# First block of an attention and convolution kernel: exponentials taken before the mean is known, their factor applied to the values and the sums

## The chip, the cores and the metric

The kernel runs on one core of a Trainium2 chip. The metric is the device time of one execution in microseconds (us). The kernel before took 1884.59 us, the median of four runs between 1883.92 and 1884.70. Engines are called TensorE (PE), VectorE (DVE), ScalarE (ACT), GpSimd (POOL) and SyncE (SP), which here only issues transfers.

## The reference

The input x has 8 images of 64 channels and 64 x 64 pixels, all in 32-bit floats. Layer 0 is an attention over the 4096 pixels of each image, with a second, unary softmax; layer 1 is a sum of three convolutions of signs (1x1, 3x3, 5x5) with a gate. What matters here is layer 0:

```python
q = einsum('oc,bcn->bon', wq, xf) + bq        # k and v alike
q = q - q.mean(axis=2);  k = k - k.mean(axis=2)
sim = softmax(einsum('bcn,bcm->bnm', q, k) / 8, axis=2)
out = einsum('bnm,bcm->bcn', sim, v)
unary = softmax(einsum('bc,bcm->bm', q_mean, k))
x = x + out + einsum('bcm,bm->bc', v, unary)
```

Inside a softmax over the keys m, a term that depends on the query n alone changes nothing, so the mean of k can be left out, and the scores are x_m . (M x_n - M mean(x)) / 8 with one product matrix M of wq and wk. Per key m, leaving out the mean multiplies every exponential by the same factor exp(x_m . M mean(x) / 8).

## The kernel before

**Tiling.** Two images lie side by side on the 128 partitions (a pair), so there are four pairs; x of a pair is a tile of 128 x 4096. The queries of a pair are cut into 8 blocks of 512 (`QB`); the 4096 keys into 32 tiles of 128. For each block and each key tile j three things happen. `scores` (L575) does four 64x64 matmuls of x against the queries q into a PSUM tile of 128 x 1024 (`ps`), and ScalarE takes the exponential of it into a tile `e`. `weighted` (L600) adds four matmuls of the value tile v against `e` to the accumulators `acc`. `summed` (L617) adds `e` to the running sums `es` on VectorE; key tiles 5, 11, 17 and 23 are instead added in DRAM by a GpSimd transfer. The convolutions of earlier blocks are mixed in between.

**Buffers.** PSUM holds two score tiles (`ps_s`), two accumulator banks (`ps_a`) and two small banks (`ps_m`, tag m). Five `e` tiles rotate (`ep`, bufs=5): an exponential needs the buffer of the tile five before it, which its weighted sum and its running sum must have left.

**Order.** Everything stands in a hand-written order (`manual_schedule`), and each engine runs its own instructions in the order in which the program lists them. `attend` (L1316) goes through the blocks: in step i it lists the scores of tile i, then the weighted sum and the running sum of tile i - 1, and then the extra steps that `plan` has put at i. Tiles whose exponentials exist already (the list `early`) skip the scores. `values` (L409) makes four value tiles at a time, with one more column for the logits of the unary softmax; `unary_part` (L435) uses them.

**The start.** x of the first pair comes in four quarters on the queues of SP and ACT (L77). TensorE meanwhile multiplies a matrix of ones (`warm`, L158), then makes M (`projection`, L160) and a key bias. When the first quarter is there, the first block's queries are made (`queries`, L536), copied without the mean by VectorE and ScalarE (`early_queries`, L346), and the scores of key tiles 0 and 1 are taken, but not their exponentials. The sums of x (`mean_part`, L296) run on VectorE and ScalarE; `mean_scores` (L312) turns them into M mean(x), `mean_scores_out` gives `mx` and `minus_mean_scores` `nmx`. `early_values` makes value tiles 0 to 3. `early_columns` (L372) makes, for each key of tiles 0 to 3, the mean's term and the unary logit; `early_exponentials` (L393) takes the exponentials of tiles 0 and 1 with the mean's term as bias, in two halves each, one per image. `mean_to_queries` (L405) subtracts the mean from the queries for the tiles after that, and `mix((first, 1), None)` makes block 1's queries.

**The end.** Sums and other denominators are tested against limits by `check` (L515), whose results are added up in `fit`; if any fails, a slower general path runs behind the main one.

Of the kernel before, what the change touches and what calls it, by code (L numbers as in the profile page):

```python
# [26 lines left out]
P = 128  # L27
C = 64
# [16 lines left out]
LOW, HIGH = 1e-20, 1e20  # L45


@with_exitstack
def conv_seq_kernel(ctx, tc, x, wqv, wk, wv, w1, w3, w5, wtap, gw, out):
# [41 lines left out]
    xt = load_x("0", slice(0, P), (nc.sync, nc.scalar, nc.sync, nc.sync))  # L91
    nc.sync.dma_start(out=wv_s, in_=wv)
# [29 lines left out]
    fit = cp.tile([P, 2, n_pairs * (NQ + 1) + 1], F32, tag="fit", name="fit")  # L122
# [47 lines left out]
    def vectors():  # L170
        nc.vector.tensor_scalar(inv, rv, BN_EPS, None, ALU.add)
        nc.vector.tensor_scalar(bv2, bv_s, 2.0, None, ALU.mult)
        nc.vector.tensor_scalar(ngb, gb_s, -1.0, None, ALU.mult)
        nc.scalar.activation(inv, inv, AF.Sqrt)

        nc.scalar.activation(lim[:, 2:3], ones[:, 0:1], AF.Exp)

# [102 lines left out]
    class Pair:  # L280
# [3 lines left out]
        def __init__(self, name, xt):  # L284
# [5 lines left out]
            self.lines = None  # L290
# [21 lines left out]
        def mean_scores(self):  # L312

            self.pm = m_tile(f"pm_{self.name}")
            for b in range(2):
                nc.tensor.matmul(
                    self.pm[img[b], 0:1], mm[img[b], img[b]], self.xm[img[b]], start=True, stop=True
                )
# [33 lines left out]
        def early_values(self):  # L352

            pv = self.pv = acc_banks(f"pv_{self.name}_e")
            for i in range(4):
                for h in range(2):
                    for b in range(2):
                        nc.tensor.matmul(
                            pv[b][img[h], i * C : (i + 1) * C],
                            self.x[img[b], bass.ds(i * P + h * H, H)],  # L360
                            self.wx[img[b], 0:C],
# [3 lines left out]

# [1373 lines left out]
```

## Time and profile before

| What | Value |
|---|---|
| median of four runs | 1884.59 us |
| the profiled execution, its time | 1884.04 us |
| its span on the core | 1882.2 us |
| granted TensorE clock | 1.0 |
| TensorE matmul busy | 1872.1 us, 99% |
| VectorE busy | 1609.2 us, 85% |
| ScalarE busy | 1265.4 us, 67% |
| exponentials of one tile (128x1024) | 1.02 us |
| running sum of one tile (128x1024) | 1.21 us |
| multiply-add on 128x512 from memory (L735) | 0.75 us |

The profile is of one execution. A row of the order of time gives the start and the duration in us, engine, line, operation, what it writes and reads, the count of instructions merged, and in brackets how long the engine was idle before and what released it. A row of the chain of waits gives the start, the duration and the instruction that the end of the kernel waited for at that time. A 32-bit matmul appears as two rows. The rows by half microseconds end with the granted clock, the share of the DMA engines and GB/s. Lines L... are those of the kernel before; the changed kernel has other numbers.

### The profile page before, as it was taken

The numbers are of one execution on the slowest core, as the hardware profiler recorded it, in microseconds if no ns is written. First come the engines' busy times: TensorE is split into PE (matmuls) and PEld (weight loads), VectorE is DVE, ScalarE is ACT, GpSimd is POOL, SyncE is SP. The second block draws the span as 40 slices with busy tenths as digits, with TensorE's granted clock in tenths as the row PEclk, the third lists the DMA queues.
The fourth block names the chain that finished last, engine by engine and source line by source line (L and its number), as shares of the span: only waits on it lengthen the run. The fifth ranks groups of instructions, "written<-read, shape, count | busy, mean of one in ns | idle before, by whom it ended". The sixth has DMA issues, their size and how long they took to land.

```text
span 1882.2 us, 51531 instructions
## 1 busy us (share of the span) xinstructions
PE 1872.1 (99%) x22076; PEld 794.4 (42%) x22076; DVE 1609.2 (85%) x2550; ACT 1265.4 (67%) x1622; POOL 130.4 (7%) x176
## 2 busy tenths in 40 slices
PE   9999999999999999999999999999999999999998
PEld 4344344443344434444434443444433444444446
DVE  7888888889888888888888898888888888888898
ACT  6666776666666676666666667666666666666664
POOL 0000000000000000000000000000000000000000
PEclk9999999999999999999999999999999999999999
DMA  4234333333333533333233343333332333333321
GB/s 126 66 62 104 82 66 72 67 58 72 68 71 78 128 81 78 67 70 71 52 81 66 89 118 83 69 70 69 72 67 59 78 75 91 89 64 78 71 51 56
DMA packets 74004, 142.81 MB, mean 76 GB/s; under 512 B 10540, under 2 KB 42152, under 8 KB 73640
## 3 DMA queue, kind: packets, MB, share of 16 engines
q0 software_dynamic: 22320, 81.27, 23.2%
q1 hardware_dynamic: 51160, 57.58, 10.4%
q8 instruction: 174, 2.85, 0.6%
q10 hardware_dynamic: 288, 0.60, 0.1%
q14 instruction: 62, 0.51, 0.1%
HBM read 39.27 MB, written 89.78 MB: 69 GB/s over the span
## 4 chain that ended last, share of the span: by engine, by line
PE 96%; DVE 2%; DMA 1%; issue 0%; ACT 0%; SPq 0%; DVEq 0%; ACTq 0%
PE ps L584 45%; PE acc L609 45%; PE z L979 2%; DVE es L627 1%; PE pv L416 1%; PE pq L565 1%; PE z L1110 0%; DMA es<-e 0%; PE z_5e L979 0%; DMA x<-in_x 0%; ACT e L597 0%; DMA e_parts<-es 0%; PE su L709 0%; PE z L1069 0%; DVE vu_lines L800 0%
## 5 line engine op out<-in xcount | busy, mean ns | idle before, releaser
L597 ACT ACTIVATE e<-ps 128x1024 f32<-128x1024 f32 (+1 forms) x1030 | 1047.5, 1017 | 564.0 <-PE ps L584 547.2
L627 DVE TENSOR_TENSOR es<-es,e 128x1024 f32<-128x1024 f32 (+1 forms) x841 | 1018.9, 1212 | 192.1 <-ACT e L597 177.6
L584 PE MATMUL ps<-q,x 64*64 64x512 f32 (+2 forms) x8448 | 1088.3, 577 | 0.8 <-DVE q L349 0.8
L609 PE MATMUL acc<-e,v 64*64 64x512 f32 (+2 forms) x8432 | 1084.3, 577 | 1.2 <-ACT e L597 1.0
L609 PEld LDWEIGHTS acc<-e,v 64*64 64x64 f32 x8432 | 333.0, 131 | 548.0 <-ACT e L597 314.9
L584 PEld LDWEIGHTS ps<-q,x 64*64 64x64 f32 x8448 | 356.2, 133 | 485.3 <-issue 263.7
L648 POOL DMA_DIRECT2D es<-e x93 | 80.1, 861 | 903.6 <-ACT e L597 598.5
L1049 DVE SCALAR_TENSOR_TENSOR sb<-pt,sb 128x256 f32<-128x256 f32 x174 | 65.9, 419 | 0.0
L979 PEld LDWEIGHTS <-wc 64*64 64x64 bf16 x3364 | 58.7, 106 | 1.7 <-issue 0.8
L648 POOL DMA_DIRECT2D es<-es x31 | 26.6, 857 | 438.6 <-DVE es L627 438.6
L625 DVE TENSOR_TENSOR es<-e,e 128x1024 f32<-128x1024 f32 (+1 forms) x31 | 37.7, 1216 | 17.2 <-ACT e L597 17.2
L979 PE MATMUL z<-ec,wc 64*64 64x128 bf16 x1392 | 51.4, 217 | 0.0
L979 PE MATMUL z<-t,wc 64*64 64x128 bf16 x1392 | 51.0, 216 | 0.1
L773 ACT ACTIVATE s<-x,wqv_s 128x512 bf16<-128x512 f32 (+2 forms) x66 | 46.2, 702 | 0.0
L1012 ACT ACTIVATE pt<-z,frac 128x256 f32<-128x256 f32 (+1 forms) x58 | 30.6, 577 | 16.9 <-PE z L979 16.9
L646 POOL DMA_DIRECT2D es<-e x31 | 17.5, 563 | 334.3 <-ACT e L597 323.1
L635 DVE COPY o<-acc 128x512 f32<-128x512 f32 (+1 forms) x32 | 22.0, 687 | 9.4 <-PE acc L609 9.3
L1023 DVE TENSOR_TENSOR pt<-pt 128x384 f32<-128x384 f32 x58 | 29.6, 552 | 0.0
L416 PEld LDWEIGHTS pv<-wx,x 64*64 64x64 f32 x992 | 21.5, 134 | 16.1 <-issue 8.6
L735 DVE SCALAR_TENSOR_TENSOR x<-x,ou,x 128x512 f32<-128x512 f32 (+2 forms) x33 | 24.3, 736 | 1.2
L663 DVE TENSOR_TENSOR e_parts<-e_parts 128x512 f32<-128x512 f32 x31 | 21.3, 688 | 3.6 <-DMA e_parts<-es 3.6
L424 ACT COPY v<-pv 128x512 f32<-128x512 f32 x31 | 18.2, 586 | 8.7 <-PE pv L416 8.7
(207 smaller groups left out, 889.9 us busy)
## 6 DMA issues: line engine op xcount, KB each, us to landing
es<-e POOLq DMA_DIRECT2D x124, 512.0 KB, 5.1
es<-es POOLq DMA_DIRECT2D x31, 512.0 KB, 5.3
e_parts<-es SPq DMA_DIRECT2D x124, 128.0 KB, 3.0
r<-rc SPq DMA_DIRECT2D x62, 128.0 KB, 2.8
out<-sb SPq DMA_DIRECT2D x29, 256.0 KB, 2.3
x<-in_x SPq DMA_DIRECT2D x24, 256.0 KB, 4.4
ec<-t SPq DMA_DIRECT2D x29, 99.0 KB, 4.4
xc<-in_x SPq DMA_DIRECT2D x30, 72.0 KB
```

Source lines behind the costliest of these rows:

```text
L416: nc.tensor.matmul(pv[img[h], b, i * w : (i + 1) * w], self.x[img[b], bass.ds((4 * g + i) * P + h * H, H)], self.wx[img[b], 0:w], start=Tr ...
L584: nc.tensor.matmul(ps[img[h], b, i * w : (i + 1) * w], self.x[img[b], bass.ds((n * j + i) * P + h * H, H)], self.q[qb][img[b], cols], star ...
L597: nc.scalar.activation(e, ps[:, :, 0 : n * w], AF.Exp, scale=1.0 / 8.0)
L609: nc.tensor.matmul(self.acc[qb][h][img[b], 0:w], self.v[img[h], t, img[b]], e[img[h], b, at : at + w], start=(t == 0), stop=(t == NK - 1),)
L625: begin.tensor_tensor(self.es[qb], self.first, e, ALU.add)
L627: nc.vector.tensor_tensor(self.es[qb], self.es[qb], e, ALU.add)
L648: nc.gpsimd.dma_start(out=out, in_=e, accum_op=ALU.add)
L773: nc.scalar.activation(sy[n][0][:, rows, pad : pad + HH], self.x2[qb][:, r0 * HH : r1 * HH].rearrange("p (h w) -> p h w", w=HH), AF.Sign, ...
L979: nc.tensor.matmul(z[img[b], :].rearrange("p (q w) -> p q w", w=HH), wc[k][img[h], n, c * C : c * C + C], src[:, first : first + step + 1 ...
L1012: nc.scalar.activation(out, z, AF.Identity, scale=frac[:, by : by + 1])
L1023: nc.vector.tensor_tensor(self.pairs[:, :, :, r, :], t[:, 0:3, 0], t[:, 0:3, 1], op)
L1049: nc.vector.scalar_tensor_tensor(out, x, by, out, ALU.mult, ALU.add, **gap)
```

## The change

The first part of x is loaded as 512 columns and the whole of x in six parts, all issued by SP; the value weights come on the ACT queue ahead of them. The exponentials of key tiles 0 to 2 are taken as soon as their scores are there, from queries without the mean; that of tile 3 stands behind the first factors in ScalarE's order. The factor of each key, exp of the mean's term, is taken later (`early_factors`), multiplied into a copy `vf` of value tiles 0 to 3 (`early_weights`), which the weighted sums of these tiles read, and into the running sums (`early_sum`). One check on the factors is added. The scores of key tile 4 are listed in the start as well. All sums of x but one run on VectorE; the last part's sum goes into the mean's matmul as a second column. Block 1's queries move to step 6 of block 0, the weight loads behind the factors, and the copies of the value weights to GpSimd. Of the warm-up matmuls 6, 2 and 3 stay of 6, 6 and 3. Blank lines are left out of the diff.

```diff
--- before.py
+++ after.py
@@ -43,6 +43,8 @@
 LOW, HIGH = 1e-20, 1e20
+EARLY = 4
+FACTOR = 1e8
@@ -88,8 +90,12 @@
     w_tap = xp.tile([P, FIRST[3], C], F32, tag="v", name="w_tap")
     nc.scalar.dma_start(out=wqv_s, in_=wqv)
     nc.sync.dma_start(out=wk_s, in_=wk)
-    xt = load_x("0", slice(0, P), (nc.sync, nc.scalar, nc.sync, nc.sync))
-    nc.sync.dma_start(out=wv_s, in_=wv)
+    nc.scalar.dma_start(out=wv_s, in_=wv)
+    xt = x_tile("0")
+    X_PARTS = [(0, 1), (1, 2), (2, 4), (4, 6), (6, 7), (7, 8)]
+    X_PARTS = [slice(a * QB, b * QB) for a, b in X_PARTS]
+    for cols in X_PARTS:
+        nc.sync.dma_start(out=xt[:, cols], in_=xf[0:P, cols])
...
@@ -167,13 +173,15 @@
         nc.tensor.matmul(t[:, 0:1], wk_s, bq_s, start=True, stop=True)
         nc.vector.tensor_copy(kb, t[:, 0:1])
+    def variances():
+        nc.vector.tensor_scalar(inv, rv, BN_EPS, None, ALU.add)
+        nc.scalar.activation(inv, inv, AF.Sqrt)
+        nc.scalar.activation(lim[:, 2:3], ones[:, 0:1], AF.Exp)
     def vectors():
-        nc.vector.tensor_scalar(inv, rv, BN_EPS, None, ALU.add)
         nc.vector.tensor_scalar(bv2, bv_s, 2.0, None, ALU.mult)
         nc.vector.tensor_scalar(ngb, gb_s, -1.0, None, ALU.mult)
-        nc.scalar.activation(inv, inv, AF.Sqrt)
-        nc.scalar.activation(lim[:, 2:3], ones[:, 0:1], AF.Exp)
@@ -287,7 +295,7 @@
-            self.lines = None
+            self.lines, self.f, self.vf = None, None, None
         def tile(self, pool, tag, i, shape=(P, QB), dtype=F32):
             return pool.tile(list(shape), dtype, tag=tag, name=f"{tag}_{self.name}_{i}")
@@ -309,13 +317,19 @@
             self.xm = self.tile(sm, "xm", 0, (P, 1))
             nc.vector.tensor_reduce(self.xm, self.xs[:, 0:parts], AX.X, ALU.add)
-        def mean_scores(self):
+        def mean_scores(self, more=()):
             self.pm = m_tile(f"pm_{self.name}")
-            for b in range(2):
-                nc.tensor.matmul(
-                    self.pm[img[b], 0:1], mm[img[b], img[b]], self.xm[img[b]], start=True, stop=True
-                )
+            cols = [self.xm] + [self.xs[:, c : c + 1] for c in more]
+            for i, col in enumerate(cols):
+                for b in range(2):
+                    nc.tensor.matmul(
+                        self.pm[img[b], 0:1],
+                        mm[img[b], img[b]],
+                        col[img[b]],
+                        start=(i == 0),
+                        stop=(i == len(cols) - 1),
+                    )
         def mean_scores_out(self):
             self.mx = self.tile(sm, "mx", 0, (P, 1))
@@ -325,22 +339,24 @@
-        def value_tiles(self):
+        def value_tiles(self, copy=nc.vector.tensor_copy):
             self.v = self.tile(xp, "v", 0, (P, NK, P))
-            wx = self.wx = self.tile(sm, "wx", 0, (P, C + 2))
+            wx = self.wx = self.tile(sm, "wx", 0, (P, C + 1))
             for b in range(2):
-                nc.vector.tensor_copy(wx[img[b], 0:C], wv_s[img[b], img[b]])
-        def value_weights(self, tiles=True):
-            if tiles:
-                self.value_tiles()
-            else:
-                nc.vector.tensor_scalar(
-                    self.wx[:, C + 1 : C + 2], self.pm[:, 0:1], -1.0 / (8 * N), None, ALU.mult
-                )
+                copy(wx[img[b], 0:C], wv_s[img[b], img[b]])
+        def value_weights(self):
+            self.value_tiles()
+            self.unary_weights()
+        def unary_weights(self):
             nc.vector.tensor_tensor(self.wx[:, C : C + 1], self.mx, kb, ALU.add)
+        def factor_weights(self):
+            self.wb = self.tile(sm, "wb", 0, (P, 1))
+            nc.vector.tensor_scalar(self.wb, self.pm[:, 0:1], -1.0 / (8 * N), None, ALU.mult)
         def early_queries(self, qb):
@@ -349,58 +365,79 @@
             nc.vector.tensor_copy(q[img[0]], self.pq[0][img[0]])
             nc.scalar.copy(q[img[1]], self.pq[1][img[1]])
-        def early_values(self):
-            pv = self.pv = acc_banks(f"pv_{self.name}_e")
-            for i in range(4):
+        def early_matmuls(self, to, tiles, weights, at):
+            for i, t in enumerate(tiles):
                 for h in range(2):
                     for b in range(2):
+                        w = weights[img[b]]
+                        n = w.shape[-1]
                         nc.tensor.matmul(
-                            pv[b][img[h], i * C : (i + 1) * C],
-                            self.x[img[b], bass.ds(i * P + h * H, H)],
-                            self.wx[img[b], 0:C],
+                            to[b][img[h], at + i * n : at + i * n + n],
+                            self.x[img[b], bass.ds(t * P + h * H, H)],
+                            w,
                             start=True,
                             stop=True,
                         )
+        def early_values(self):
+            self.pv = acc_banks(f"pv_{self.name}_e")
+            self.early_matmuls(self.pv, range(EARLY), self.wx[:, 0:C], 0)
         def early_values_out(self):
             for b in range(2):
                 nc.scalar.copy(
-                    self.v[:, 0:4, img[b]], self.pv[b][:, 0 : 4 * C].rearrange("p (t c) -> p t c", c=C)
+                    self.v[:, 0:EARLY, img[b]],
+                    self.pv[b][:, 0 : EARLY * C].rearrange("p (t c) -> p t c", c=C),
                 )
-        def early_columns(self, i0):
-            if i0 == 0:
-                self.add = self.tile(sm, "add", 0, (P, 2, 4, 2))
-            pb = misc_banks(f"pb_{self.name}_e{i0}")
-            for i in range(2):
-                for h in range(2):
-                    for b in range(2):
-                        nc.tensor.matmul(
-                            pb[b][img[h], 2 * i : 2 * i + 2],
-                            self.x[img[b], bass.ds((i0 + i) * P + h * H, H)],
-                            self.wx[img[b], C : C + 2],
-                            start=True,
-                            stop=True,
-                        )
+        def early_columns(self, i):
+            if i == 0:
+                self.f = self.tile(sm, "add", 0, (P, 2, EARLY))
+                self.pb = acc_banks(f"pb_{self.name}_e")
+            else:
+                self.pb = misc_banks(f"pb_{self.name}_e")
+            self.early_matmuls(self.pb, range(i, i + 2), self.wb, 0)
+        def early_exponential(self, ps, j):
+            e = ep.tile([P, 2, QB], F32, tag="e", name=f"e_{self.name}_e{j}")
+            nc.scalar.activation(e, ps, AF.Exp, scale=1.0 / 8.0)
+            return e
+        def early_factors(self, i):
             for b in range(2):
-                nc.vector.tensor_copy(
-                    self.add[:, b, i0 : i0 + 2], pb[b][:, 0:4].rearrange("p (t c) -> p t c", c=2)
-                )
-        def early_exponentials(self, ps, j):
-            e = ep.tile([P, 2, QB], F32, tag="e", name=f"e_{self.name}_e{j}")
-            for b in range(2):
-                nc.scalar.activation(
-                    e[:, b, :], ps[:, b, :], AF.Exp, scale=1.0 / 8.0, bias=self.add[:, b, j, 1:2]
-                )
-            return e
+                nc.scalar.activation(self.f[:, b, i : i + 2], self.pb[b][:, 0:2], AF.Exp)
         def early_unary(self):
             self.eu = self.tile(sm, "eu", 0, (P, 2, NK))
-            nc.scalar.activation(self.eu[:, :, 0:4], self.add[:, :, :, 0], AF.Exp)
+            for b in range(2):
+                nc.scalar.activation(self.eu[:, b, 0:EARLY], self.pb[b][:, 2 : 2 + EARLY], AF.Exp)
+        def early_weights(self, i):
+            if i == 0:
+                self.vf = self.tile(fp, "r", "vf", (P, EARLY, P))
+            nc.vector.tensor_tensor(
+                self.vf[:, i : i + 2, :].rearrange("p t (b c) -> p b t c", b=2),
+                self.v[:, i : i + 2, :].rearrange("p t (b c) -> p b t c", b=2),
+                self.f[:, :, i : i + 2].unsqueeze(3).broadcast_to([P, 2, 2, C]),
+                ALU.mult,
+            )
+        def early_sum(self, qb, j, e):
+            if j == 0:
+                self.es[qb] = self.tile(sm, "es", qb, (P, 2, QB))
+            es = self.es[qb]
+            for b in range(2):
+                f = self.f[:, b, j : j + 1]
+                if j == 0:
+                    nc.vector.tensor_scalar(es[:, b, :], e[:, b, :], f, None, ALU.mult)
+                else:
+                    nc.vector.scalar_tensor_tensor(
+                        es[:, b, :], e[:, b, :], f, es[:, b, :], ALU.mult, ALU.add
+                    )
@@ -512,7 +549,12 @@
-        def check(self, r, i, sides=(0, 1)):
+        def check_factors(self):
+            self.check(self.f.rearrange("p b t -> p (b t)"), n_pairs * (NQ + 1) + 1, high=FACTOR)
+        def check(self, r, i, sides=(0, 1), high=None):
             w = r.shape[-1]
             for side in sides:
@@ -525,7 +567,7 @@
                     r,
                     AF.Sign,
                     bias=lim[:, side : side + 1],
-                    scale=1.0 - 2.0 * side,
+                    scale=(1.0, -HIGH / high)[side] if high else 1.0 - 2.0 * side,
                     accum_out=fit[:, side, i : i + 1],
                 )
@@ -600,6 +642,7 @@
         def weighted(self, qb, j, e, part=(slice(0, QB), 1)):
             cols, n = part
             w = cols.stop - cols.start
+            v = self.vf if self.early(qb, j) else self.v
             if j == 0:
                 self.acc[qb] = acc_banks(f"acc_{self.name}_{qb}_{cols.start}")
             for t in range(n * j, n * j + n):
@@ -608,15 +651,21 @@
                     for h in range(2):
                         nc.tensor.matmul(
                             self.acc[qb][h][img[b], 0:w],
-                            self.v[img[h], t, img[b]],
+                            v[img[h], t, img[b]],
                             e[img[h], b, at : at + w],
                             start=(t == 0),
                             stop=(t == NK - 1),
                         )
+        def early(self, qb, j):
+            return self.vf is not None and qb == 0 and j < EARLY
         def summed(self, qb, j, e, dram=False, begin=nc.vector):
-            if dram and j in DRAM_TILES:
+            if self.early(qb, j):
+                self.early_sum(qb, j, e)
+            elif dram and j in DRAM_TILES:
                 self.add_in_dram(qb, e, j == DRAM_TILES[0])
             elif j == 0:
                 self.first = e
@@ -1405,7 +1454,10 @@
                 for i in range(NQ):
                     if i > 0:
                         put(4 * i - 1, pairs[0].values, i)
-                    put(4 * i + 1, pairs[0].unary_part, i)
+                    put(4 * i + 1 if i > 0 else 5, pairs[0].unary_part, i)
+                put(1, pairs[0].early_weights, 2)
+                put(6, lambda: mix((pairs[0], 1), None))
+                put(10, pairs[0].check_factors)
...
@@ -1580,37 +1632,45 @@
     with tc.manual_schedule():
         first = Pair("0", xt)
+        first.value_tiles(nc.gpsimd.tensor_copy)
+        variances()
         warm(6)
         projection()
-        vectors()
         key_bias()
-        warm(6)
-        first.mean_part(0, quarters[0])
+        warm(2)
+        first.mean_part(0, X_PARTS[0])
         first.query_tiles(0, score_tiles)
         for b in range(2):
             first.queries(0, b)
+        warm(3)
+        first.mean_part(1, X_PARTS[1], True)
         first.early_queries(0)
-        early = [first.scores(0, j, exp=False) for j in range(2)]
-        first.mean_part(1, quarters[1], True)
-        first.mean_part(2, quarters[2])
-        for c in range(2):
-            first.mean_part(3 + c, slice(N * (6 + c) // 8, N * (7 + c) // 8), c == 1)
-        first.value_tiles()
+        early = [first.scores(0, j) for j in range(2)]
         first.early_values()
+        early.append(first.scores(0, 2))
+        first.early_values_out()
+        last = first.scores(0, 3, exp=False)
+        for c in range(2, 5):
+            first.mean_part(c, X_PARTS[c])
+        first.mean_sum(5)
+        first.mean_part(5, X_PARTS[5])
+        first.mean_scores((5,))
+        first.factor_weights()
+        first.mean_scores_out()
+        first.mean_to_queries(0)
+        first.early_columns(0)
+        first.early_factors(0)
+        early.append(first.early_exponential(last, 3))
+        first.unary_weights()
+        first.minus_mean_scores()
+        first.early_columns(2)
+        first.early_matmuls(first.pb, range(EARLY), first.wx[:, C : C + 1], 2)
+        first.early_factors(2)
+        early.append(first.scores(0, 4))
+        first.early_unary()
+        first.early_weights(0)
         load_weights()
-        first.mean_sum(5)
-        first.mean_scores()
-        first.mean_scores_out()
-        warm(3)
-        first.early_values_out()
-        first.value_weights(False)
-        first.minus_mean_scores()
-        first.early_columns(0)
-        early = [first.early_exponentials(ps, j) for j, ps in enumerate(early)]
-        first.mean_to_queries(0)
-        first.early_columns(2)
-        first.early_unary()
-        mix((first, 1), None)
+        vectors()
         good = attend([first] + [None] * (n_pairs - 1), early)
```

More of the change, by code (lines that the diff above doesn't have):

```diff
@@ L120, in conv_seq_kernel @@
     rec = cp.tile([P, 8], F32, tag="rec", name="rec")
-    fit = cp.tile([P, 2, n_pairs * (NQ + 1) + 1], F32, tag="fit", name="fit")
+    fit = cp.tile([P, 2, n_pairs * (NQ + 1) + 2], F32, tag="fit", name="fit")
     lim = cp.tile([P, 3], F32, tag="lim", name="lim")
@@ L1529, in attend @@
         nc.vector.tensor_reduce(nb_, fit, AX.XY, ALU.add)
-        nc.vector.tensor_scalar(nb_, nb_, n_pairs * (16.0 * NQ + 2.0) - 16.0 + 2 * QB, None, ALU.is_equal)
+        nc.vector.tensor_scalar(nb_, nb_, n_pairs * (16.0 * NQ + 2.0) - 16.0 + 2 * QB + 4.0 * EARLY, None, ALU.is_equal)
         p.signs_wide(b, 2, r0, r1, None)
```

## The prediction

> **What bounds the kernel now.** I read the page's head first, then the chain of waits, then the order of time of the first 15 us, then the arrival of x.
>
> ```profile
> span 1882.2 us, 51531 instructions
> PE 1872.1 (99%) x22076; PEld 794.4 (42%) x22076; DVE 1609.2 (85%) x2550; ACT 1265.4 (67%) x1622; POOL 130.4 (7%) x176
> PE 96%; DVE 2%; DMA 1%; issue 0%; ACT 0%; SPq 0%; DVEq 0%; ACTq 0%
> ```
>
> TensorE is busy for 99% of the span and carries 96% of the chain. A change at the start is worth what it takes out of the stretch before TensorE runs without gaps, plus the real matmuls that it moves into that stretch. The chain of the first 40 us shows where the gapless stretch begins and what a step costs:
>
> ```profile
> 1.20 5.47 DMA x<-in_x
> 8.56 1.95 PE ps L584 x16
> 12.31 0.52 PE pb_e L381 x16
> 13.76 0.71 PE pq L537 x2
> ...
> 20.53 0.86 PE acc L609 x8
> 21.39 0.86 PE ps L584 x8
> 26.54 0.46 PE pv L416 x32
> 27.00 0.91 PE ps L584 x8
> ```
>
> From 13.76 us matmuls follow each other; a tile's scores or its weighted sum costs 0.86 us, a group of four value tiles 0.46. Check: between 13.76 and 27.00 (the start of score tile 8) stand block 1's queries, weighted sums 0 to 6, scores 2 to 7 and two value groups: 13 x 0.86 + 2 x 0.46 + about 0.86 = 12.96 of 13.24 us, so only 0.28 us is gap. The order of time shows what the stretch before consists of:
>
> ```profile
> 4.45 0.29 DVE L163 COPY mm<-mm_p 128x128 f32<-128x128 f32 x1 [3.43 <-PE mm_p L162]
> 6.72 1.08 PE L537 MATMUL pq<-x,mm 64*64 64x512 f32 x4 [0.31 <-DMA x<-in_x]
> 7.87 0.58 ACT L350 COPY q<-pq 64x512 f32<-64x512 f32 x1 [1.30 <-PE pq L537]
> 10.47 0.85 PE L358 MATMUL pv_e<-wx,x 64*64 64x64 f32 x29
> 11.52 0.16 DVE L322 TENSOR_SCALAR mx<-pm 128x1 f32<-128x1 f32 x1 [0.57 <-PE pm L316]
> 12.96 0.48 DVE L407 TENSOR_SCALAR q<-q,mx 128x512 f32<-128x512 f32 x1
> 13.01 2.42 ACT L396 ACTIVATE e_e<-ps,add 128x512 f32<-128x512 f32 x4 [0.94 <-DVE add L389]
> ```
>
> The first quarter of x starts the queries at 6.72, the mean is there at 11.52, and no exponential starts before it. The arrival of x, by half microseconds and by its issues:
>
> ```profile
> 3.00:3.50 0.50, 0.50 (x4) 0.50 (x4) 0.00 (x0) 0.00 (x0) 0.00 (x0) 1.00 1.04 328
> 8.00:8.50 0.50, 0.00 (x0) 0.00 (x0) 0.50 (x2) 0.47 (x2) 0.00 (x0) 1.00 0.84 323
> 9.00:9.50 0.50, 0.50 (x12) 0.18 (x8) 0.50 (x1) 0.50 (x2) 0.00 (x0) 1.00 0.07 22
> ...
> DMA to landing us min/median/max: 5.5/6.5/7.5
> ```
>
> The last column is GB/s: bytes flow from about 2 us to 9.1 us whatever their order, 2.3 MB in all. So the mean cannot come much sooner; what can come sooner is the work that needs 512 columns.
>
> **The change, part by part.**
>
> *x in six parts on SP alone.* Adding the GB/s of the half-microsecond windows, the 468 KB of weights and first 512 columns are through at 3.6 us, the next 512 columns (731 KB) at 4.4, all of x at 9.1. Landings trail the bytes: in before the first quarter needed about 1.18 MB (two queues sharing), through at 5.6, and landed at 6.67; the last was in use at 9.63. With 0.5 to 1.0 us of trailing the first part lands at 4.1 to 4.6, the second at 4.9 to 5.4 (I take 5.3), the last at 9.5. SP issues six at about 0.43 us each, done by 4 us; the weight loads behind them move from 10.8 to about 13.7, and their first reader stands at 27.9. Free.
>
> *Scores early.* The queries now wait for the product matrix (copied by 4.74), not for x: 4.9 to 6.0. ScalarE's order puts the sum of part 1 ahead of its half of the query copy: 5.3 + 0.63 + 0.19, then 0.58 gives 6.75, and behind it wait all scores. Scores 0: 6.8 to 7.9; scores 1 to 8.8; early values 0.85 to 9.6 (their weights come by GpSimd, off the path). Exponentials 0 and 1 (one 128x1024 each, 1.02) end at 9.0 and 10.0 and free the two score buffers: scores 2 at 9.6 to 10.5, scores 3 to 11.4, exponential 2 until 11.6.
>
> *The mean.* VectorE: three parts (1.21, 1.21, 0.69) behind their landings end near 10.1, the last part 0.69 near 10.8. Its matmuls stand behind scores 3 in TensorE's order, so they start at 11.4, not 10.8: four instead of two, 0.5 to the first reader, mean at 11.85 against 11.52. This is the step where ScalarE and TensorE, not the data, decide.
>
> *The factors.* Factor weight, mean, queries (0.48), unary weight, negative mean: five VectorE steps from 11.85 to 12.8. First factor columns on TensorE 12.15 to 12.7 (row: 16 matmuls 0.52). The second factor columns take the buffer of the mean's matmul, which is free only after the negative mean: 12.9 to 13.4. Then 16 more unary columns, 32 matmul rows like the early values' 0.85: to 14.25. Only then scores 4, and the gapless stretch: 14.25 against 13.76, later by 0.5. Weighted sum 0 follows at 15.1; its scaled values (128x256, nearest row 0.43) are ready at 13.6, two small factor exponentials having run at 12.7. The second factors run behind exponential 3 (13.0 to 14.05) and are needed for weighted sum 2 at 16.8. Covered.
>
> *Sums with the factor.* Three 1.22 additions (3.7) become two multiplications and six multiply-adds on 128x512: 2 x 0.48 + 6 x 0.75 = 5.5, and 2 x 0.43 for the scaled values: VectorE does 2.7 us more. It begins at 13.2, ends tile 3 near 19.5 and tile 4 at 20.8, where before tile 4 ended at 22.9. The five exponential buffers come free in time (exponential 8 at about 25 needs tile 3's). Free; if VectorE fell 4 us behind, exponentials would wait and each us would count.
>
> *Sum.* From scores 4 at 14.25 to the start of scores 8 stand weighted sums 0 to 6, scores 4 to 7, two value groups, queries: 11 x 0.86 + 0.92 + 0.86 = 11.24, with the same 0.28 of gap 25.77, against 27.00: 1.2 us gained. Scores 2 and 3 give 1.72, the later start takes 0.5. Without the gap (less waits on late exponentials) it would be 1.5; I take 1.4. Two small checks on ScalarE (0.3 to 0.5 each, 67% busy) are free. From scores 8 on both run the same order. The end is untouched.
>
> *Ends of the unknowns.* The second part lands between 4.4 (its bytes) and 6.67 (before's first quarter, which had as many bytes ahead on SP): the chain moves by -0.3 (then the product matrix holds it) to +1.35 us. The gap in the new stretch lies between none and twice the old, 0.56. Gain from 0 to 1.9; if the mean's matmuls slipped in at 10.85, 2.0.
>
> The profiled execution took 1884.04 (span 1882.2 and 1.84 around it); less 1.4 is 1882.6. It lies 0.55 under the median of 1884.59, so for the median 1883.2.
>
> [...] Row: before's four loads of 512 KB issued within 1.4 us keep 320 to 400 GB/s, also after 6 us when the ACT queue is empty. [...]
>
> **The rivals.**
>
> *A. The second part is late (slower side of my forecast).* The copy of the queries waits behind a sum of columns it has no need of. At 6.67 the gain is about 0: 1884.5. Break-even is a slip of 1.4 us; for: landings of 5.5 us after issue in before; against: half the bytes.
>
> *B. Given back in the block.* The 2.7 us of VectorE or the crossed factor steps stall weighted sums: gain 0 to a loss of 1, 1884.6 to 1885.6. Against: the buffer count above.
>
> *C. Slower by over 0.2%: TensorE slow at the start.* The first 12 warm-up matmuls take 2.93 us, the second 12 take 1.60 (0.244 and 0.133 each) while the granted clock reads 1.00 throughout. Of fifteen warm-up matmuls eleven stay (6+6+3 become 6+2+3; each is two rows). If the slow pace (factor 1.83) held from 4.9 on: queries end 6.9, scores 0 at 9.7, scores 3 at 15.9, mean matmuls 4.5 to 5 us late and the columns 1.1 more: about 4.5 us slower, 1889. It passes 0.2% from 5.2 us of slip. Against: the fast pace was there at 4.80, before any of the removed matmuls ran. [...]
>
> *D. Faster by over 0.2%.* If nothing but the data held it: the last part's bytes at 9.1, 0.69 for its sum, and the 2.85 us from the mean's matmuls (11.4) to scores 4 (14.25). The stretch would start at 12.6, 1.6 earlier than I put it, and the gain be 1.4 + 1.6 = 3.0: short of 3.8.
>
> **How the numbers follow.** 0.2% is 3.8 us, about what a measurement of this kernel tells from no change. Forecast 0.55 (1882.2 to 1884.0), A 0.18, B 0.15, C and unnamed stalls 0.08, more than forecast 0.04. Forecast, A and B lie within 0.2%: 0.88; faster 0.04, slower 0.08. The range runs from the gain's end with 0.9 for the scatter of four runs and the chip, 1881.7, to B's end, 1886.0.
>
> **What would show it.** In the profile after: queries at 4.9 to 6.0; three exponentials ended by 11.7; the mean at about 11.85, its matmuls behind scores 3 and not behind the last sum; scores 4 at 14.25; scores 8 at 25.6 to 25.8; from there the same chain. Wrong if the second part lands after 6.7, if exponentials of tiles 5 to 9 wait for VectorE, or if matmuls before 11 us take twice their time.

## The result, and the profile after

The changed kernel takes 1886.89 us at the median of 38 runs (1884.63 to 1889.92), the kernel before beside it 1884.22 us (58 runs, 1883.48 to 1887.3). The ratio is 1.0015, with a 95% interval of 1.0011 to 1.0020: slower by 2.7 us. Forecast were 1883.2 us, with 1881.7 to 1886.0 as the range. The loss is within the 0.2% that were called "the same", but it has the other sign and lies outside the range. The profiled execution took 1888.09 us, 4.05 more than that of before.

The page of the changed kernel, its head and its chain by engine:

```profile
span 1886.3 us, 51601 instructions
PE 1875.4 (99%) x22104; PEld 795.9 (42%) x22104; DVE 1613.6 (86%) x2553; ACT 1264.9 (67%) x1627; POOL 130.6 (7%) x178
...
PE 90%; DVE 1%; DMA 0%; ACT 0%; issue 0%; DVEq 0%; ACTq 0%
```

TensorE is still the bound. It has 28 matmuls and 28 weight loads more; that number will matter. The order of time of the changed kernel's start on TensorE (start, duration, both in us):

```profile
5.95 1.97 PE L579 MATMUL pq<-x,mm 64*64 64x512 f32 x4
7.86 1.65 PE L164 MATMUL warm<-ones 128*128 128x128 f32 x6
9.43 2.09 PE L626 MATMUL ps<-q,x 64*64 64x512 f32 x16
11.81 2.00 PE L626 MATMUL ps<-q,x 64*64 64x512 f32 x16
14.34 1.14 PE L374 MATMUL pb_e<-wb,x 64*64 64x1 f32 x29 [0.34 <-DVE mx L336]
15.76 0.62 PE L626 MATMUL ps<-q,x 64*64 64x512 f32 x1
16.68 4.50 PE L652 MATMUL acc<-e,r_vf 64*64 64x512 f32 x24
```

The queries' four rows take 1.97 us where the kernel before took 1.08, and six warm-up rows 1.65 instead of 0.94. Scores 0 stand at 9.43 instead of the forecast 6.8, scores 4 at 15.76 instead of 14.25, scores 8 at 28.83 instead of 25.6 to 25.8. Behind the mean, 24 rows of weighted sums take 4.50 us. The rows by half microseconds (after the duration the busy time of PE, PEld, DVE, ACT and POOL, then granted clock, DMA share, GB/s) say why for this last part:

```profile
16.00:16.50 0.50, 0.50 (x9) 0.27 (x6) 0.50 (x2) 0.31 (x3) 0.00 (x0) 1.00 0.00 0
16.50:17.00 0.50, 0.50 (x8) 0.32 (x4) 0.50 (x3) 0.00 (x0) 0.00 (x0) 0.60 0.00 0
19.50:20.00 0.50, 0.50 (x7) 0.18 (x3) 0.50 (x2) 0.00 (x0) 0.00 (x0) 0.50 1.02 310
20.00:20.50 0.50, 0.50 (x9) 0.26 (x5) 0.50 (x2) 0.00 (x0) 0.00 (x0) 0.99 0.96 294
```

The granted clock is 0.50 from 16.6 to 20.0 us. For the early slowness the same column is no witness. It prints 1.00 there (in the window from 9.00 to 9.50 us, for one), but the trace holds no clock record before 9.77 us (the kernel before: none before 4.30), so the 1.00 there says nothing of the pace.

The start is only half of it. As milestones I take the VectorE copy of the weighted sum at the end of each of the 32 blocks. Against the kernel before, the changed kernel is 2.0 us late at the end of block 0, 2.5 at the end of block 2, 2.1 from block 19 to block 30, 3.2 at the copy of block 31, and 4.1 at the end of the span. Two later places therefore lose time as well. The chain of waits in block 2, first of the changed kernel, then of the kernel before:

```profile
152.29 8.00 DMA es<-e
160.40 1.03 ACT e L639
161.48 1.09 PE acc L652 x8
```

```profile
150.57 0.86 PE acc L609 x8
151.43 0.86 PE ps L584 x8
```

An exponential waits for its buffer, which GpSimd's accumulating transfer still reads. In the kernel before, this stretch of the chain is TensorE alone; there too an exponential waits for that transfer, 1.14 us at 157.94, but TensorE loses nothing by it. And VectorE in the last block, where it is the bound, in the same order:

```profile
1815.74 0.69 DVE L712 TENSOR_TENSOR e_parts<-e_parts 128x512 f32<-128x512 f32 x1 [1.03 <-DMA e_parts<-es]
```

```profile
1812.54 0.69 DVE L663 TENSOR_TENSOR e_parts<-e_parts 128x512 f32<-128x512 f32 x1
```

The kernel before has no wait at that instruction. The parts come late because the send of the running sums ahead of them lands late, and the page's list of DMA issues (count, KB each, median us from issue to landing) shows that this is so in most blocks, again first after, then before:

```profile
es<-es POOLq DMA_DIRECT2D x31, 512.0 KB, 6.0
```

```profile
es<-es POOLq DMA_DIRECT2D x31, 512.0 KB, 5.3
```

Nothing in that send was changed. This is the riddle that most of the experiments went to.

### The profile page after: what moved, and what is told of

It reads as the page before. It is cut to its first block, busy times and chain, and to the rows that moved or that the text cites. A ratio compares the mean times of both kernels' runs of the same rounds, so it can differ in the third digit from the quotient of the medians.

```text
span 1886.3 us, 51601 instructions
## 1 busy us (share of the span) xinstructions
PE 1875.4 (99%) x22104; PEld 795.9 (42%) x22104; DVE 1613.6 (86%) x2553; ACT 1264.9 (67%) x1627; POOL 130.6 (7%) x178
## 3 DMA queue, kind: packets, MB, share of 16 engines
q8 instruction: 175, 2.87, 0.6%
## 4 chain that ended last, share of the span: by engine, by line
PE 90%; DVE 1%; DMA 0%; ACT 0%; issue 0%; DVEq 0%; ACTq 0%
PE acc L652 43%; PE ps L626 43%; PE z L1028 2%; DVE es L676 1%; PE pv L453 1%; PE pq L607 1%; DMA es<-e 0%; PE z L1159 0%; PE z_5e L1028 0%; ACT e L639 0%; PE su L758 0%; PE z L1118 0%; DVE es_j L1178 0%; DVE vu_lines L849 0%; PE po L500 0%
```

## The experiments

The first group came from the theory that the pace of TensorE at the start, and nothing else, costs the time. The theories of the program's fetches (F) and of the loads of x (S) were formed from its traces.

**1. Filling the wait behind the mean.** Two warm-up matmuls behind the mean's matmul and two behind exponential 3 of the changed kernel:

```diff
+        wt_ = warm(2)      # behind mean_scores
+        warm(2, wt_)       # behind early_exponential(last, 3)
```

> Changed kernel with four warm-up matmuls put back where TensorE waits after the mean (two behind the mean's matmuls, two behind the first factor columns). Theory 1 (pace of TensorE: the granted clock was 0.50 from 16.65 to 20.0 us in the changed kernel's profile, after 2 us of one-column matmuls and waits): the drop to 0.50 is gone, scores 8 start about 1.5 us earlier than 28.8, the median falls from 1886.9 to about 1885.4. Rival (the new order itself is too long: ScalarE's part sum ahead of the query copy, the factor columns, VectorE's factor sums; the pace is only a mark): median stays at 1886.9 or rises by the 0.5 us of added matmuls, drop or no drop.

Measured: 1888.41 us, ratio 1.0015 (1.0006 to 1.0024). The start came out as wanted:

```profile
5.85 1.08 PE L580 MATMUL pq<-x,mm 64*64 64x512 f32 x4 [0.16 <-DMA x<-in_x]
6.86 0.94 PE L164 MATMUL warm<-ones 128*128 128x128 f32 x6
15.52 2.84 PE L653 MATMUL acc<-e,r_vf 64*64 64x512 f32 x24
26.00 1.09 PE L627 MATMUL ps<-q,x 64*64 64x512 f32 x8
```

There is no fall to 0.50, scores 8 start at 26.00, and block 0 ends 0.8 us before the kernel before. Yet the span is 3.4 us longer than before's: 1.5 go in block 2, 2.3 in the last block, 0.7 behind it. So the theory of the pace, which explains the head, does not explain the time.

**2 and 3. More warm-up at the start, alone and with the filling.** `warm(2)` behind `key_bias()` becomes `warm(6)` again.

> Changed kernel with six instead of two warm-up matmuls behind the key bias, as before the change. Theory 1 in its second place (queries at 5.95 took 1.97 us, and matmuls stayed at about 0.25 us a row until about 9.8): more work there makes the array fast by 5 to 6.5 us in more executions; queries take about 1.1, scores 0 start near 7.5 instead of 9.4, median about 1885.5. Rival (when the pace rises depends on the moment at which the kernel starts, not on these matmuls): same pace as without, median 1886.9 or up to 0.8 us more, since the queries start later.

> Both additions. Theory 1: drop gone and early pace up, scores 4 at about 14.3 and scores 8 near 26, median 1883.5 to 1884, level with or below the kernel before. Rival (order too long): 1886.5 to 1887.5.

Measured: 1889.21 us, ratio 1.0020 (1.0011 to 1.0029), and 1890.62 us, ratio 1.0026 (1.0016 to 1.0036). Theory 1 had expected both to be faster than the changed kernel; they are the two slowest of all. The twelve rows take 2.69 and 2.52 us, for the most part at the slow pace, and push the queries to 7.41 and 7.24; there is no fall to 0.50 in either trace. The send lands in 6.3 and 6.4 us.

**4. The kernel before with less warm-up** (6, 2 and none of its 6, 6 and 3):

> The kernel before with warm-up matmuls 6, 2 and none instead of 6, 6 and 3, nothing else. Theory 1: the pace alone makes the loss: slow queries and scores and a drop to 0.50 within the first 25 us, 1.5 to 3 us slower than before. Rival: the kernel before has the quarter of x at 6.7 to wait for, so nothing changes, within 0.5 us of 1884.2.

Measured: 1888.05 us, ratio 1.0017 (1.0008 to 1.0026). Block 0 ends 0.4 us earlier than before's; the loss comes later, 0.5 us in block 18, 0.1 to 0.3 in each of blocks 24 to 28, where TensorE falls behind within 5 us of a block's end, 0.2 in the last block and 0.9 behind it. What causes these losses was not settled, and neither theory 1 nor its rival had expected them. The send lands in 5.4 us. A change of seven warm-up matmuls in the first 12 us moves things at 1460 us: that is what pointed to the program itself.

**What the traces then showed.** The page's queue "q8 instruction" moved 174 packets and 2.85 MB before, 175 and 2.87 MB after: 16 KB each. Before has 2 x 22076 rows of matmuls and weight loads, 253.7 to a packet; from the start of one packet to that of the next, 256 of the rows start at the median, in either trace (153 to 360 in nine of ten cases before, 120 to 390 after). The packets begin between 13.2 and 1880.5 us in the kernel before and take 1.05 us each at the mean, as the page counts the time of one of the 16 DMA engines. I take it that TensorE's program comes in these pieces of 256 instructions all through the run, and that where the fetches fall against the work hangs on how many instructions TensorE has ahead. Runs 5 to 8 test that. Two answers on the DMA queues, for the same 3.2 us of block 13's send (1.2 to 4.4 us after its issue); first the changed kernel, whose send lands in 6.2 us, then the kernel before, where it lands in 5.0:

```profile
q0 software_dynamic: 132, 0.51, 98.9%
q8 instruction: 1, 0.02, 1.8%
```

```profile
q0 software_dynamic: 136, 0.52, 94.2%
```

In the changed kernel a fetch lies in the send, and the send's last packet ends 1 us later than the bulk. In the kernel before it came 3.9 us ahead of the send and again at its end. In blocks 4 and 6 of the second and the third pair it is the other way round: there the send of before takes 6.0 to 6.3 us, and that of after 5.1 to 5.3. Of the 403 sends in the thirteen traces, the 154 in which a fetch begins 0.3 to 4.4 us after the issue land in 6.2 us at the median, the other 249 in 5.3.

**5 and 6. More instructions for the kernel before, and the control.** A helper issues small matmuls that nothing waits for, of two instructions each; the 32-bit `warm` has four.

```diff
+    def pad(n):
+        t = m_tile("warm")
+        w = ones.bitcast(BF16)
+        for i in range(n):
+            h = i % 2
+            nc.tensor.matmul(t[img[h], 0:C], w[img[h], 0:C], w[img[h], 0:C], start=True, stop=True)
-        warm(6)
+        warm(3)
+        pad(36)            # the control: pad(6)
         projection()
```

> The kernel before, with the first six warm matmuls replaced by three of them and 36 small ones (64x64, 64 columns, bf16) that nothing waits for: 60 instructions of TensorE more, at a place where TensorE waits for the weights' load anyway. Layout, loads and the rest of the program stay those of before. Theory F (the fetches of TensorE's own program): the queue "q8 instruction" moved 174 packets of 16 KB in the kernel before for 44152 records of TensorE (matmuls and weight loads), so one fetch per 256 records, each about 1 us on one of the DMA engines; the changed kernel has 56 records more ahead of block 0's end, so every later fetch comes about a quarter of a piece earlier against the work, and falls into the send of the running sums. F expects here what the changed kernel shows: the send (es<-es) lands in 6.0 to 6.3 us at the median of the issues, against 5.3 before; block 2 loses 0.4 to 1.5, the last block 1 to 2.4, and the time is 1.5 to 3 us above the kernel before. Theory L (the changed kernel's layout of the buffers, or its two more loads on SyncE's queue, slow the send): neither is here, so 5.3 us, no new wait in the last block, and the time within 0.7 us of the kernel before.

> The kernel before, with the first six warm matmuls replaced by three of them and 6 small ones: the count of TensorE's records is exactly that of before. It is the control for the run with 36: the head has less warm work, but the fetches stand where they did. F: the send lands in 5.3 us, no block after block 0 loses anything against before, and the time is within 0.7 us of before. If instead it is 1.5 us or more slower, the missing warm work at the start costs by itself, and the run with 36 says nothing.

Measured: 1887.62 us, ratio 1.0011 (1.0002 to 1.0020), and 1886.56 us, ratio 1.0005 (0.9996 to 1.0014). The page and VectorE's last block of the run with 36:

```profile
es<-es POOLq DMA_DIRECT2D x31, 512.0 KB, 6.1
```

```profile
1816.37 0.69 DVE L670 TENSOR_TENSOR e_parts<-e_parts 128x512 f32<-128x512 f32 x1 [0.69 <-DMA e_parts<-es]
```

The kernel before, with its own layout and loads, has the slow send of the changed kernel, slow in most of the blocks where the changed kernel's is slow, and fast (5.2 to 5.5) in blocks 4 and 6 of the first three pairs. In its trace it loses 1.9 us in block 0, whose pace rose late (first clock record at 9.81 us), 1.0 in block 2, 0.8 in the last block and 0.8 behind it. The control keeps the pattern of before (5.4) and after block 0 stays within 0.2 us; its 1.3 us go in block 0 alone, where the pace rose late, with the first clock record at 9.18 us. Its median is 1.0 us above before, against 0.7 expected, and 1.1 below that of the run with 36. Theory L (layout or loads) falls.

**7 and 8. The fetches put back.** The warm-up groups of the changed kernel, and of the first experiment's kernel, become small matmuls, so that both have 255 instructions more than before, one short of a whole piece:

```diff
-        warm(6)  ...  warm(2)  ...  warm(3)
+        pad(74)  ...  pad(24)  ...  pad(22)     # the other: 70, 20, 22
```

> The changed kernel, its three groups of warm matmuls ahead of the first scores (6, 2 and 3) replaced by 74, 24 and 22 small ones: 196 records more, so that with its own 59 instructions more it stands 255 behind before, one short of a whole piece of 256: the fetches fall where before has them. Layout and loads are those of the changed kernel. F: the send lands in 5.3 to 5.4 us at the median, block 2 and the last block lose nothing against before, and what remains of the loss is that of the head (0 to +2 us by the end of block 0, as the pace at the start comes out). L: 6.0 us and the losses of the changed kernel, +0.4 in block 2 and +1.1 to 2 at the end.

> The changed kernel with the four warm matmuls behind the mean's (the run whose head was 0.8 us ahead of before, and which lost 1.4 in block 2, 2.3 in the last block and 0.7 at the end), its earlier warm groups replaced by 70, 20 and 22 small ones: 255 records more than before. F: the send lands in 5.3 to 5.4 us, no loss behind block 0, and the time is 0.5 to 1 us below the kernel before, or equal to it where the head's pace comes late. L: the send stays at 6.2 us, and the time 2.5 to 3 us above the kernel before.

Measured: 1885.60 us, ratio 1.0001 (0.9992 to 1.0010), and 1886.12 us, ratio 1.0003 (0.9994 to 1.0012). The page and the last block of the first of them:

```profile
es<-es POOLq DMA_DIRECT2D x31, 512.0 KB, 5.4
```

```profile
1814.21 0.69 DVE L719 TENSOR_TENSOR e_parts<-e_parts 128x512 f32<-128x512 f32 x1
```

The control's pattern is back, in blocks 4 and 6 as in the others, and the wait in the last block is gone (the last block now loses 0.2 us in either). With the fetches moved, and its warm-up of small matmuls, the filled kernel went from a ratio of 1.0015 to 1.0003; the intervals overlap, and it is the traces that show the send and the wait to be mended. But block 2 still lost 1.4 and 1.2 us, against theory F, which had expected nothing there. The run with 70 was expected 0.5 to 1 us below before and came out 0.6 above.

**9, 10 and 11. Block 2.** In that block SyncE issues six 256 KB loads of the next pair's x in a row, and GpSimd's accumulating transfer (512 KB) follows. The lead of the loads on the transfer, its landing and the loss of block 2 against the kernel before, in us:

| kernel | lead | landing | lost in block 2 |
|---|---|---|---|
| before | 3.5 | 7.6 | 0 |
| changed | 3.4 | 8.0 | 0.5 |
| before, same count | 3.3 | 7.5 | 0.0 |
| before, less warm-up | 3.1 | 7.5 | 0.0 |
| before, 36 more | 3.0 | 8.6 | 1.0 |
| changed, second trace | 3.0 | 9.0 | 1.4 |
| changed, refilled | 2.8 | 8.9 | 1.4 |
| changed, refilled and filled | 2.9 | 8.8 | 1.2 |
| changed, filled | 2.2 | 9.0 | 1.5 |
| changed, both (run 3) | 2.0 | 8.7 | 1.1 |
| changed, more warm-up | 1.7 | 9.6 | 2.0 |

With a lead of 3.1 or more at most 0.5 is lost, with 3.0 or less 1.0 to 2.0. The lead hangs on landings of tenths of a microsecond in the block before: SyncE's queue holds the loads (issued from 146.75 us on in the kernel before) behind the spreading of the reciprocals (145.59), which waits for the parts of block 1. The edit, in the refilled and filled kernel (run 8) and in the kernel before; the changed kernel itself ran beside them:

```diff
-                        put(9 + 2 * c, load, bass.ts(c, N // 8))
+                        put(9 + 2 * c if c < 4 else 17 + c, load, bass.ts(c, N // 8))
```

> The changed kernel with the mean's wait filled and the fetches put back (the run that came out level with before), and with the eight 256 KB loads of the next pair's x issued as four and four instead of six and two. Its only large loss left was 1.2 us in block 2, where the exponential waits for its buffer until GpSimd's accumulating DMA has landed. Theory S (the six loads of x on SyncE's queue share the DMA engines with that transfer: the later they start before it, the more it is stretched): with four loads in the first group the second accumulating DMA of block 2 lands in 7 us or less, the loss in block 2 falls from 1.2 us to 0.4 or less, and the time comes to 0.3 to 1.2 us below the kernel before. Rival T (the fetches of the program stretch it): the fetches stand where they did, so block 2 loses 1.2 again.

> The kernel before with the same four and four loads of x. In its trace the accumulating DMA of block 2 was not on the chain, so S and T both expect nothing: the time within 0.7 us of before, the milestones of the blocks within 0.3. Were it faster by 1 us or more, the gain of the other run would not be that of the changed kernel's block 2.

> The changed kernel unaltered, beside the two others on one chip, with a second trace. Theory F: its send of the running sums lands in 6.0 us again, slow in the same blocks, and the last block loses 1 to 2.4 us. Its head varies by the clock: where the granted clock falls to 0.50 behind the mean, block 0 ends about 2 us late, where it doesn't, 0 to 1. The time is 2 to 3.5 us above the kernel before.

Measured: 1884.74 us, ratio 0.9996 (0.9987 to 1.0005); 1884.65 us, ratio 0.9996 (0.9987 to 1.0005); 1888.52 us, ratio 1.0013 (1.0004 to 1.0022). ScalarE's waits from 148 to 172 us (what for, us in all, times, longest) in the changed kernel's second trace, and in the kernel with four and four:

```profile
ACT e L639 <- PE ps L626: 6.3, 10, 0.8
ACT e L639 <- DMA es<-e: 2.6, 1, 2.6
```

```profile
ACT e L647 <- PE ps L634: 7.7, 12, 0.8
```

With four loads ahead the transfer lands in 5.5 us (6.1 in the kernel before), the wait is gone and block 2 loses nothing (-0.1). The count of instructions ahead was the same and a fetch still fell into the transfer, 4.7 us after its issue, so theory S holds and its rival falls. The changed kernel so mended is 0.7 us below the kernel before, the kernel before with the same edit 0.8, both within the measurement. The latter was expected within 0.7 us; in its trace the milestones lie 0.2 to 0.4 us behind before's, so the trace shows no cause for the 0.8. No gain of the change itself is shown.

**A loss in block 0 that no experiment touched.** In run 9's trace scores 8 start 0.3 us before those of the kernel before, and yet block 0 ends 0.4 late. The exponential of key tile 10 waits there for the buffer that tile 5 had; the chain of waits of run 9, its row, and the row of the kernel before:

```profile
22.51 9.25 DMA es<-e
```

```profile
31.87 1.02 ACT L647 ACTIVATE e<-ps 128x1024 f32<-128x1024 f32 x1 [1.45 <-DMA es<-e]
31.46 1.02 ACT L597 ACTIVATE e<-ps 128x1024 f32<-128x1024 f32 x1 [0.74 <-PE ps L584]
```

This is the transfer that takes the exponentials of key tile 5 to DRAM. It lands in 7.2 to 9.4 us in all eight traces of the changed kernel and its variants, in 4.3 to 5.2 in the five of the kernel before and its variants. The loads of the weights, which the change moved, and those behind them in SyncE's queue still run beside it: SyncE issues the first of them at 14.1 to 16.2 us there, at 10.6 to 12.7 here. In runs 2, 3, 7, 8 and 9 the exponential waits 1.0 to 1.6 us, and TensorE loses 0.2 to 0.8. In the changed kernel's own two traces, where the clock fell, TensorE came too late to be held. That the moved loads are the cause was not tested by putting them back.

## Why the prediction was wrong

**The head: mechanism right, two terms missing.** Where TensorE ran at full pace from 5.2 us on (the first experiment), scores 8 started at 26.00 against 26.82 in the same view of the kernel before (its chain of waits, on which the forecast of 25.6 to 25.8 was built, has 27.00), and block 0 ended 0.8 us early. With a pace that rose late in both, at 10.7 us in run 7 and 9.2 in the control of run 6, scores 8 start 1.2 us ahead of the control's. The step of two more score tiles ahead of the mean thus does nearly what it was costed at, 0.8 to 1.2 us of 1.4. The order was as forecast as well: the mean's matmuls stand behind scores 3, and the VectorE work called "Free" (2.7 us) delayed no exponential.

**"Against: the fast pace was there at 4.80" is the step that failed first.** It took the moment at which the pace rises in one execution for a property of the kernel. The last of the prediction's own signs of being wrong, matmuls before 11 us at twice their time, is what the profile shows. The first clock record lies at 4.30 us in before's trace, at 4.2 to 10.7 in the others, and it does not order by the warm-up issued (the kernel before with four and four: 4.2; with its warm-up cut to 6 and 2: 5.9; with three warm and six small matmuls: 9.2). The slow pace of rival C did come. Its price is smaller than the 4.5 us worked out: among the changed kernels without a fall of the clock, scores 8 started 0.8 us early with a record at 5.2 (run 1), 0.6 early at 7.4 (run 8), 0.3 early at 8.9 (run 9) and 0.1 late at 10.7 (run 7). Runs 2 and 3, whose twelve rows push the queries back, start them 0.1 and 0.5 late with records at 7.1 and 6.8.

**A term that no row of before had: the fall to 0.50.** The 3.41 us at 0.50 cost 1.7 us: the 24 rows of weighted sums behind the mean take 4.50 us, in run 1, without the fall, 2.84. It follows a stretch of one-column matmuls and waits, 13.6 to 15.8 us, that the change makes. The mean granted clock of an execution tells roughly how often it comes; roughly, because the last 2.6 us of the profiled execution are at 0.50 as well and count in it. In 27 of 40 executions, and in 8 of the 11 of run 11, it is 0.998; the 27 take 1888.5 us at the median. In the other 13 it is 0.999, and these take 1885.55. The 2.9 us between the two groups are more than the 1.7 of the fall; what else parts them has no trace, since both traces of the changed kernel have the fall. Of the kernels that fill the stretch with matmuls (runs 1, 3, 8 and 9) none of 42 executions shows 0.998; with more warm-up at the start alone (run 2) 5 of 11 do, and of the kernel before without its warm-up behind the mean (run 4) 3 of 11 show 0.998 or less. But run 7, which leaves the stretch unfilled, has none in 11 either. So the filling goes with the absence of the fall; what else decides it was not settled. In both traces of the changed kernel the fall starts 6.83 us after the first record; what sets this, and the 3.41 us for which it lasts in the first of them, no run shows.

**The first two parts of x.** The first was put at 4.1 to 4.6, so that the queries would wait for the product matrix; it landed at 5.2, and at 5.8 in the first experiment, where the queries waited for it until 5.85 instead of starting at 4.9. The second was put at 5.3 and landed at 6.2, within the ends given. In this execution it cost nothing, since the queries ended later still; in the first experiment it held ScalarE's copy until 7.28, as rival A describes. The two loads more cost the mean nothing: the last part landed at 9.5, as forecast.

**"Free" for the weight loads** looked at their first reader alone. They also meet the transfer of key tile 5, and in five of the six traces of changed kernels without a fall of the clock 0.2 to 0.8 us of block 0 go there.

**"From scores 8 on both run the same order. The end is untouched."** The order is the same and the sentence is still wrong, by 2 us. Two things are not in the order of the instructions: where in the stream the program's fetches fall, and the tenths by which transfers on different queues miss each other. The 56 instructions more moved the fetches (in block 13 from 4.5 us after the send's issue to 3.9), the send of the running sums took 6.0 us instead of 5.3, and in the last block, where VectorE is the bound, that cost 1.1 us; in block 2 the loads of x met the accumulating transfer, 0.5 us in one trace and 1.4 in the other.

**The sum.** In the profile: head +2.0, block 2 +0.5, block 19 -0.4, last block +1.1, end +0.9, together the 4.1 us by which the span grew. The -0.4 is a stall of the kernel before that the changed kernel lacks, and the 0.9 behind the last copy weren't tested. With the fall of the clock, block 2 and the last block mended by experiments (run 9), the median is 0.7 us below the kernel before, within the measurement, and the control gets as much without the change: of the forecast 1.4 us nothing is shown in the time.

## What to carry to other kernels

In a kernel at 99% of one engine, a change at the start need not be over when the order of the work is the same again: here it shifted the fetches of the program and the meetings of transfers by tenths, the send of the running sums went from 5.3 to 6.0 us, and VectorE waited 1.03 us up to 1815.74 us. Before a loss of some tenths of a per cent is put down to the edit, compare milestones block by block and the landing times of transfers that were not changed, and run a control that alters only the count of instructions. Ask of a moved load not only when its reader comes, but what other transfer it now meets. Where a burst of loads stretches a transfer that holds a buffer, try to split it: here six loads ahead meant 7.5 to 9.6 us, four meant 5.5 to 6.1.

## What the runs showed of the hardware

- The queue "q8 instruction" moved 16 KB packets all through the run, 174 before and 175 after, of 1.05 and 1.03 us each at the mean, and 256 of TensorE's rows started at the median between one and the next; that they are TensorE's program is my reading. The 512 KB send landed in 6.2 us at the median where such a fetch began 0.3 to 4.4 us after its issue (154 of 403 sends), in 5.3 in the others. 60 instructions more in the kernel before took the median of its 31 sends from 5.3 to 6.1 us, 196 more in the changed kernel from 6.0 to 5.4.
- The pace of TensorE did not rise at the same time in the thirteen traces: the first clock record lay between 4.2 and 10.7 us, and not in the order of the warm-up issued. Before it the profile's clock column shows 1.00 while matmuls took almost twice their time (1.97 against 1.08 us for the queries).
- The 512 KB accumulating transfer of GpSimd in block 2 landed in 7.5 to 8.0 us where it started 3.1 to 3.5 us after the first of six 256 KB loads, in 8.6 to 9.6 at 1.7 to 3.0 us after it; 2.9 to 3.1 us after the first of four loads, in 5.5 to 6.1.
